# Four edits to the placing of small work in a graph-attention layer: late edges of heavy tiles, a third early q row, a bias column on ScalarE, earlier scans in a sort

## The chip, the cores and the metric

The kernel runs on one core of a Trainium2 chip. The metric is the device time of one execution in microseconds. A core has TensorE (PE: matmuls and transposes), VectorE (DVE), ScalarE (ACT), GpSimd (POOL: here mostly the issue of indirect DMAs, which gather or scatter rows by index) and SyncE (SP: issue of plain DMAs). Each engine works through its own queue of instructions, and semaphores order work between engines.

## The reference

One transformer layer on a sparse graph, in f32, with a residual and a last layer norm around it:

```python
hs = layer_norm(x); ht = layer_norm(h_target)            # 4096 x 512 each
q = (ht @ Wq + bq).reshape(T, 8, 64) / 8.0
k = (hs @ Wk + bk).reshape(S, 8, 64); v = (hs @ Wv + bv).reshape(S, 8, 64)
logits = where(adj[None] != 0, einsum('thd,shd->hts', q, k), -1e30)
ctx = einsum('hts,shd->thd', softmax(logits), v).reshape(T, 512)
h = layer_norm(ht + ctx @ Wo + bo)
h = h + gelu(h @ W1) @ W2                                 # 512 -> 2048 -> 512
out = layer_norm(x + h)
```

`adj` is 4096 x 4096 int32. It holds the diagonal and about 0.4% of other entries, so a target row has 11 to 39 neighbours.

## The kernel before, in words

**Lists instead of dense attention.** The kernel never multiplies 4096 x 4096. For each tile of 128 targets `edges(i)` reads the tile's rows of `adj` in four quarters (SP loads them; ScalarE L740 turns a quarter into flags and counts degrees; VectorE L747 multiplies by a column index and L749 takes maxima of short segments into `cand`, the last of them noted in `maxima`). Then VectorE L756 to L773 decode the candidates into `gid` and take the 24 (`RE`) largest into the target's record `rec`. What stays in `gid` is written to a DRAM table `rest_d` by SP (L780, in `keep_rest`).

**Sorting by degree.** `sort(part)` sorts the records of one half of the targets by falling or rising number of edges: a one-hot matrix (L841), totals on PE (L853), running sums on VectorE (two scans, L859), ranks by a triangular matmul on PE (L870) and VectorE L871 to L874, then 16 scatters by POOL (L878) that write the records to DRAM in sorted order. So every tile of 128 sorted targets has a `cap`, the largest degree in it: 11, 13, 14, 15, 15, 16, 17, 17, 18, 19, 19, 20, 22, 23, 24, 39, then 12, 38, 13, 24 and so on to 18. Tiles 15 and 17, with caps 39 and 38, are the only ones above `RE`: they are the heavy tiles. For them `rest_of(i)` gathers the leftovers back from `rest_d` (POOL, L992, into a new `gid`), and VectorE takes further edges from it, eight at a time (L792 clears those already taken, L793 takes the next eight, twice over), then counts them (L796, L799). `issue(k)` starts `rest_of` when the tile's first gathers are issued, and finishes it before the gathers beyond slot 12.

**Stage 1** (0 to about 276 us). `project` normalises the source rows in 16 groups of 256, transposes them and multiplies by Wk and Wv (L954), and the K|V rows go to a DRAM table `kvd`. Beside it run the lists of the first half, `late_constants` (constants with the biases; PE L662 makes a transposed row, VectorE L665 copies one column of it to `rbc`, which PE uses in a further matmul) and `sort(0)`. At its end `first_fronts` makes the q rows of the first `EARLY` tiles: `front(i)` gathers the targets' rows of `h_target` (L992), normalises (ScalarE L1023), transposes (PE L1035, ScalarE L1038), multiplies by Wq (PE L1045, eight matmuls) and adds the bias (VectorE L1050). For later tiles the same `front` is stepped inside attention, with a VectorE tie (L1027) that keeps it behind the newest logits, and L1030 and L1031 in place of L1025 and L1023.

**Stage 2.** `attention` goes through the 32 tiles in groups of two or one, and through a tile's edges three slots at a time. A slot is one neighbour of each of the 128 targets: POOL gathers its K|V rows (L992) into a ring of 17, later 20 slots. VectorE multiplies keys by q (L1285) and sums per head (L1291), ScalarE takes exp (L1298, L1313, L1263), VectorE weights two slots' values (L1232) and, in some tiles, adds two slots (L1236), ScalarE weights the third (L1266 x8), and PE adds all up by transposing matmuls into PSUM (L1245). `finish` closes a tile (sums L1121 to L1128, ScalarE L1131, PE L1137 to L1155, layer norm with POOL's power L692, ScalarE L1177, PE L1186, ScalarE L1190). `feed` runs the feed-forward network on PE (L1405, L1414) with gelu on ScalarE (L1408). `other_lists` makes the lists of the second half and `sort(1)` in the background.

**What sets the order.** All streams are Python generators; `_weave` interleaves them by the costs that they yield, which gives a program order. A list scheduler of the tile framework then reorders each engine's queue before the kernel runs, so the order on the chip is fixed at build time. `behind(x)` pins what is issued inside it after the last of the instructions in the list `x`: `issues` holds the newest gather, `logits` the newest L1291, `maxima` the newest L749, `newest` the newest ScalarE L1266.

Of the kernel before, what the change touches and what calls it, by code (L numbers as in the profile page):

```python
# [375 lines left out]
MAXE = 40  # L376
RE = 24
DEG, TGT, ROW, RST, E0 = 0, 1, 2, 3, 5
# [65 lines left out]
def adj_resnorm_kernel(  # L444
# [88 lines left out]
    with tc.tile_pool(name="keep", bufs=1) as keep:  # L533
# [17 lines left out]
        with ExitStack() as late:  # L551
# [89 lines left out]
            def late_constants():  # L641


                zero = wp.tile([P, 2 * D // P], F32, name="zero")
                nc.vector.memset(zero, 0.0)
                nc.sync.dma_start(kvd[0:1, :].rearrange("o (p n) -> (o p) n", p=P), zero)
                nc.sync.dma_start(wo, Wo.rearrange("(c p) n -> p c n", p=P))
                nc.sync.dma_start(wq, Wq.rearrange("(c p) n -> p c n", p=P))
                bob = row_bcast(wp, bo, "bob")
                nc.sync.dma_start(bqr, bass.AP(tensor=bq.tensor, offset=bq.offset,  # L650
                                               ap=[[0, P], [1, D]]))
                yield
                yield
                pb = psi.tile([P, D], F32, name="pq", bufs=3)
                for kc in range(KC):
                    nc.tensor.matmul(pb, bvc[:, kc:kc + 1].to_broadcast([P, P]), wo[:, kc, :],
                                     start=kc == 0, stop=kc == KC - 1)
                nc.vector.tensor_add(bob, pb, bob)
                yield
                pt = psi.tile([P, D], F32, name="pq", bufs=3)  # L660
                for kc in range(KC):
                    nc.tensor.transpose(pt[:, kc * P:(kc + 1) * P], bob[:, kc * P:(kc + 1) * P],  # L662
                                        ident)
                rbc = wp.tile([P, KC], F32, name="rbc")
                nc.vector.tensor_copy(rbc.unsqueeze(2), pt.rearrange("p (c t) -> p c t", c=KC)  # L665
                                      [:, :, 0:1])
                nc.vector.tensor_add(b1r, rbc, b1c)
                yield
                pb = psi.tile([P, D], F32, name="pq", bufs=3)
                for kc in range(KC):  # L670
                    nc.tensor.matmul(pb, rbc[:, kc:kc + 1].to_broadcast([P, P]), wq[:, kc, :],
                                     start=kc == 0, stop=kc == KC - 1)
                nc.vector.tensor_sub(bqr, bqr, pb)
                nc.vector.tensor_scalar_mul(bqr, bqr, HD ** -0.5)
# [48 lines left out]
            def behind(ins):  # L723
                return tc.issue_after(ins[-1]) if ins else nullcontext()
# [57 lines left out]
            def rest_of(i):  # L782


                keep_rest()
                rec = recs[i]
                gid = lp.tile([P, 2 * SEG, 8], F32, name="gid")
                flat = gid.rearrange("p s e -> p (s e)")
                gather(flat, rest_d, rec[:, TGT:TGT + 1])
                yield  # L790
                for c in range(E0 + RE, E0 + MAXE, 8):
                    nc.vector.match_replace(flat, rec[:, c - 8:c], flat, 0.0)  # L792
                    nc.vector.max(rec[:, c:c + 8], flat)  # L793
                has = lp.tile([P, MAXE], F32, name="ehas")
                num = lp.tile([P, 1], F32, name="num")
                nc.vector.tensor_scalar(has, rec[:, E0:E0 + MAXE], 0.0, 0.0, op0=ALU.is_gt,  # L796
                                        op1=ALU.add, accum_out=num)
                part = 1 if TILES[i][0] >= PARTS[1][0] * P else 0
                nc.vector.tensor_tensor(bad[:, 6 + part:7 + part], num, rec[:, DEG:DEG + 1],  # L799
                                        ALU.not_equal)  # L800
# [20 lines left out]
            def sort(part):  # L821

                i0, n = PARTS[part]
                me = slice(i0, i0 + n)
                pool, R = lp, Rs[part]
                nc.vector.tensor_reduce(deg[:, me], dpart[:, me, :], AX.X, ALU.add)
                nc.vector.tensor_copy(R[:, :, DEG], deg[:, me])
                dif, rank = tools[:, 928:928 + n], tools[:, 944:944 + n]
                ranki, b16 = tools[:, 960:960 + n].bitcast(I32), tools[:, 976:984].bitcast(BF16)
                nc.vector.scalar_tensor_tensor(dif, deg[:, me], float(RE), cnt[:, me], op0=ALU.min,  # L830
                                               op1=ALU.not_equal)
                nc.vector.tensor_reduce(bad[:, 1 + part:2 + part], dif, AX.X, ALU.max)
                nc.vector.tensor_scalar(dif, deg[:, me], 0.0, float(NB - 1), op0=ALU.max,
                                        op1=ALU.min)
                nc.vector.tensor_scalar(b16, dif, -1.0, float(NB - 1), op0=ALU.mult, op1=ALU.add)
                if part:
                    oh = turn_of("wide", wide).bitcast(BF16)
                else:
                    oh = wp.tile([P, NB * n], BF16, name="oh")
                oh = oh[:, :NB * n].rearrange("p (b i) -> p b i", b=NB)  # L840
                nc.vector.tensor_tensor(oh, b16.unsqueeze(1).to_broadcast([P, NB, n]),  # L841
                                        bins.unsqueeze(2).to_broadcast([P, NB, n]), ALU.is_equal)
                ohf = oh.rearrange("p b i -> p (b i)")
                pos = turn_of("wide", wide).bitcast(F32)
                pos = pos[:, :NB * n].rearrange("p (b i) -> p b i", b=NB)
                posf = pos.rearrange("p b i -> p (b i)")
                w = NB * n // 2
                yield 6.0 if part else 2.0
                tots = []
                for c in range(2):  # L850
                    sl = slice(c * w, (c + 1) * w)
                    pt = ps.tile([P, w], F32, name="t" if part else "cps", bufs=2)
                    nc.tensor.matmul(pt, ones_bf, ohf[:, sl], start=True, stop=True)  # L853
                    tots.append((sl, pt))
                if not part:
                    yield 6.0
                for c, (sl, pt) in enumerate(tots):
                    with behind([] if part else maxima):
                        scan = nc.vector.tensor_tensor_scan(  # L859
                            posf[:, sl], one_c.to_broadcast([P, w]), pt,  # L860
                            0.0 if c == 0 else posf[:, c * w - 1:c * w],
                            op0=ALU.mult, op1=ALU.add)
                while factors:
                    with behind([scan.ins]):
                        factors.pop()()
                yield 4.0
                for c in range(2):
                    sl = slice(c * w, (c + 1) * w)
                    pa = ps.tile([P, w], F32, name="t" if part else "cps", bufs=2)
                    nc.tensor.matmul(pa, lower, ohf[:, sl], start=True, stop=True)  # L870
                    nc.vector.tensor_add(posf[:, sl], pa, posf[:, sl])  # L871
                nc.vector.tensor_mul(pos, pos, oh)
                nc.vector.tensor_reduce(rank, pos.rearrange("p b i -> p i b"), AX.X, ALU.add)
                nc.vector.tensor_copy(ranki, rank)  # L874
                yield 10.0
                for i in range(n):
                    with behind(issues):
                        ins = nc.gpsimd.indirect_dma_start(  # L878
                            out=recs_d[part][:, :],
                            out_offset=bass.IndirectOffsetOnAxis(ap=ranki[:, i:i + 1], axis=0),  # L880
                            in_=R[:, i, :], in_offset=None)

                    tc.declare_no_dep(ins.ins, group=f"scatter{part}", reason="other rows")
                    tc.add_to_no_dep_group(f"scatter{part}", ins.ins)
                    yield 4.5 if part else 1.3
                done.add(part)
# [104 lines left out]
            def gather(dst, table, idx):  # L991
                issues[:] = [nc.gpsimd.indirect_dma_start(  # L992
                    out=dst, out_offset=None, in_=table[:, :],
                    in_offset=bass.IndirectOffsetOnAxis(ap=idx, axis=0)).ins]
# [56 lines left out]
                                               op0=ALU.mult, op1=ALU.add)  # L1051
                tqs[i] = tq

            EARLY = 2

            SG = [(i, j0, min(S, cap - j0)) for i, (_, cap) in enumerate(TILES)
                  for j0 in range(0, cap, S)]
# [524 lines left out]
```

## Time and profile before

| what | value |
|---|---|
| three runs | 1753.59, 1755.61, 1753.04 us (median 1753.59) |
| profiled execution, own time | 1754.37 us |
| its span | 1752.6 us |
| granted TensorE clock, mean | 0.978 |
| busy: PE, DVE, ACT, POOL | 1651.9, 1425.2, 1236.1, 1020.6 us |
| kv gathers (POOL L992) | 603, 784.7 us busy, 1301 ns each |
| matmuls of the feed (L1405, L1414) | 468.8 and 464.8 us busy |
| first feed matmul starts at | 321.42 us |

All positions in microseconds below are counted from the start of the span. In a timeline a line gives start, duration, engine, source line, operation, result and operands, number of instructions; the bracket holds the idle time of that engine just before, and what ended it. In the list of waits a line gives who waited for whom, then the total in us, the number of times and the longest. In the page's 40 slices each digit is a tenth of busy share.

### The profile page before, as it was taken

To read this page: it belongs to the slowest core of one execution; us is meant where nothing else is said; L and a number is where in the kernel's file an instruction comes from. 1 tells how busy PE (TensorE), PEld (TensorE's weight loads), DVE (VectorE), ACT (ScalarE), POOL (GpSimd) and SP (SyncE) were. 2 spreads that over 40 slices of the span, in tenths; PEclk is the share of its full clock that TensorE was granted. 3 is DMA by queue.
4 is the path that set the end of the run, shared out by engine and by line. 5 is a ranking of instruction groups with operands and counts; after the bars stand their busy time and mean duration, and the time that the engine had idled before them with its cause. 6 is when DMAs were issued, how large, how long until landed. Compare 5 with 4: busy or idle time off the path is not lost. (4 is left out here: it accounts for less than half of the span.)

```text
span 1752.6 us, 22726 instructions
## 1 busy us (share of the span) xinstructions
PE 1651.9 (94%) x6978; PEld 1078.3 (62%) x6978; DVE 1425.2 (81%) x2456; ACT 1236.1 (71%) x3135; POOL 1020.6 (58%) x824
## 2 busy tenths in 40 slices
PE   7999996899999999898889999999999999999997
PEld 3444443676676767565567677666666666666665
DVE  6888797889898988997888998988988788999300
ACT  5776663788678977685668888787868677878311
POOL 1000155757666666778777788777887856775101
PEclk9999997999999999998999999999999999999999
DMA  9999988978888887777788888887777767675000
GB/s 353 370 389 361 370 264 286 372 259 284 296 291 297 303 321 256 241 223 246 251 303 292 296 277 314 287 275 237 266 243 242 254 220 257 223 259 191 24 1 27
DMA packets 141610, 461.00 MB, mean 263 GB/s; under 512 B 18036, under 2 KB 23048, under 8 KB 141480
## 3 DMA queue, kind: packets, MB, share of 16 engines
q0 software_dynamic: 96272, 342.33, 57.5%
q1 hardware_dynamic: 39504, 98.26, 15.7%
q10 hardware_dynamic: 5704, 18.89, 2.7%
q8 instruction: 57, 0.93, 0.2%
q14 instruction: 73, 0.60, 0.1%
HBM read 430.61 MB, written 28.79 MB: 262 GB/s over the span
## 5 line engine op out<-in xcount | busy, mean ns | idle before, releaser
L992 POOL DMA_INDIRECT kv<-kvd,rec x603 | 784.7, 1301 | 302.7 <-issue 113.4
L1405 PE MATMUL pf<-h2T,w 128*128 128x256 f32 (+1 forms) x2304 | 468.8, 358 | 5.4 <-ACT h2T L1190 5.4
L1414 PE MATMUL po<-w,gt 128*128 128x512 f32 x1024 | 464.8, 597 | 5.8 <-ACT gt L1408 5.8
L1405 PEld LDWEIGHTS pf<-h2T,w 128*128 128x128 f32 x2304 | 394.4, 191 | 67.0 <-issue 17.9
L1285 DVE TENSOR_TENSOR kv<-kv,tq 128x1536 f32<-128x1536 f32 (+2 forms) x211 | 351.8, 1678 | 54.9 <-DMA kv<-kvd,rec 39.6
L1266 ACT ACTIVATE kv<-kv,pa 128x64 f32<-128x64 f32 x1520 | 390.2, 337 | 3.8
L1291 DVE TENSOR_REDUCE lg<-kv 128x24 f32<-128x1536 f32 (+2 forms) x211 | 350.6, 1669 | 0.4
L1414 PEld LDWEIGHTS po<-w,gt 128*128 128x128 f32 x1024 | 189.1, 192 | 203.9 <-issue 194.6
L1245 PEld LDWEIGHTS cps<-ident,kv 128*128 128x128 f32 x1828 | 219.3, 145 | 112.3 <-issue 46.4
L1245 PE MATMUL cps<-ident,kv 128*128 128x128 f32 x1828 | 244.3, 280 | 45.0 <-DVE kv L1236 24.8
L1232 DVE TENSOR_TENSOR kv<-kv,p 128x1024 f32<-128x1024 f32 (+1 forms) x211 | 251.3, 1195 | 23.9 <-ACT p L1298 22.5
L692 POOL TENSOR_TENSOR n_rs<-n_ve,mhalf 128x2 f32<-128x2 f32 (+2 forms) x53 | 53.8, 1014 | 328.6 <-DVE n_ve L685 155.0
L740 ACT ACTIVATE kv<-kv 128x1024 uint8<-128x1024 int32 x128 | 134.4, 1053 | 61.0 <-DMA kv<-in_adj_dram 22.1
L1408 ACT ACT_TABLE_LOAD x109 | 139.8, 1283 | 1.9
L1408 ACT ACTIVATE gt<-pf 128x512 f32<-128x512 f32 x128 | 76.4, 597 | 75.5 <-PE pf L1405 72.1
L954 PE MATMUL pq<-wk,h2T 128*128 128x512 f32 x256 | 119.5, 609 | 2.5 <-DMA wk<-in_L_gnn_Wk_dram 1.1
L1155 PE MATMUL t<-wo,rb 128*128 128x512 f32 x256 | 117.4, 602 | 4.5 <-DVE rb L1142 4.5
L954 PE MATMUL pq<-wv,h2T 128*128 128x512 f32 x256 | 115.6, 594 | 4.7 <-DVE rbc L665 3.0
L1045 PE MATMUL t<-wq,tq 128*128 128x512 f32 x256 | 115.1, 593 | 1.2 <-ACT tq L1038 1.2
L749 DVE MAX8 cand<-kv 128x8 uint16<-128x171 uint16 (+1 forms) x384 | 108.5, 325 | 1.1
L1298 ACT ACTIVATE p<-lg 128x24 f32<-128x24 f32 (+2 forms) x179 | 39.0, 218 | 82.2 <-DVE lg L1291 79.3
L954 PEld LDWEIGHTS pq<-wv,h2T 128*128 128x128 f32 x256 | 48.4, 190 | 68.0 <-issue 56.5
(165 smaller groups left out, 1593.9 us busy)
## 6 DMA issues: line engine op xcount, KB each, us to landing
kv<-in_adj_dram SPq DMA_DIRECT2D x128, 512.0 KB, 7.0
kvd<-tq ACTq DMA_DIRECT2D x23, 512.0 KB, 6.8
kv<-kvd,rec POOLq DMA_INDIRECT x603, 5.9
kv<-in_L_gnn_h_target_dram SPq DMA_DIRECT2D x32, 256.0 KB, 7.1
w<-in_L_gnn_W_dram SPq DMA_DIRECT2D x8, 1024.0 KB, 8.4
kv<-in_x_dram SPq DMA_DIRECT2D x15, 512.0 KB, 8.4
kvd<-kv ACTq DMA_DIRECT2D x9, 512.0 KB, 6.8
rest_d<-gid SPq DMA_DIRECT2D x32, 96.0 KB, 4.7
```

The source lines that it names most:

```text
L740: nc.scalar.activation(sg, a, AF.Sign, accum_out=dpart[:, i, h:h + 1])
L954: nc.tensor.matmul(pkv, hT[:, kc, j * P:(j + 1) * P], w[:, kc, :], start=kc == 0, stop=kc == KC - 1)
L992: issues[:] = [nc.gpsimd.indirect_dma_start(out=dst, out_offset=None, in_=table[:, :], in_offset=bass.IndirectOffsetOnAxis(ap=idx, axis=0) ...
L1155: nc.tensor.matmul(pa, ct[:, c, :], wo[:, c, :], start=False, stop=c == KC - 1, skip_group_check=True)
L1232: nc.vector.tensor_tensor(v4, v4, p[:, j0:j0 + m, :].unsqueeze(3) .to_broadcast([P, m, H, HD]), ALU.mult)
L1245: nc.tensor.matmul(cps[:, c, :], kv[:, j, D + c * P:D + (c + 1) * P], ident, is_transpose=True, start=j0 + j == 0 and c == 0, stop=j0 + n ...
L1266: newest[:] = [nc.scalar.mul(v, v, pa[:, hd:hd + 1]).ins]
L1285: nc.vector.tensor_tensor(kv[:, :n, :D], kv[:, :n, :D], tq[:, :D].unsqueeze(1) .to_broadcast([P, n, D]), ALU.mult)
L1291: logits[:] = [nc.vector.tensor_reduce(lg[:, :n, :], kv[:, :n, :D].rearrange("p j (h d) -> p j h d", h=H), AX.X, ALU.add).ins]
L1405: nc.tensor.matmul(pf[:, k, :], w1[(f0 + k) // KC][:, kc, (f0 + k) % KC * P:((f0 + k) % KC + 1) * P], h2T[:, kc, :w], start=kc == 0, stop= ...
L1408: nc.scalar.activation(gt, pf, AF.Gelu_apprx_tanh)
L1414: nc.tensor.matmul(po[j], gt[:, k, j * P:(j + 1) * P], w2[(f0 + k) // KC][:, (f0 + k) % KC, :], start=False, stop=f0 + k == FC - 1, skip_g ...
```

## The change

1. The column copy of L665 goes from VectorE to ScalarE.
2. In `rest_of`, the gather of the leftovers is pinned behind the newest gather, and the loop of L792 and L793 behind the newest logits. (In program order they stood there already; before, the scheduler could move them ahead.)
3. In `sort(0)`, the list `maxima` is copied one step sooner, when the totals are multiplied, and the scans are pinned behind that older entry.
4. `EARLY` goes from 2 to 3: the third tile's q row is made in `first_fronts`, with the first two.

```diff
@@ late_constants
-                nc.vector.tensor_copy(rbc.unsqueeze(2), pt.rearrange("p (c t) -> p c t", c=KC)
+                nc.scalar.copy(rbc.unsqueeze(2), pt.rearrange("p (c t) -> p c t", c=KC)
                                       [:, :, 0:1])
@@ rest_of
-                gather(flat, rest_d, rec[:, TGT:TGT + 1])
-                yield
-                for c in range(E0 + RE, E0 + MAXE, 8):
-                    nc.vector.match_replace(flat, rec[:, c - 8:c], flat, 0.0)
-                    nc.vector.max(rec[:, c:c + 8], flat)
+                with behind(issues):
+                    gather(flat, rest_d, rec[:, TGT:TGT + 1])
+                yield
+                with behind(logits):
+                    for c in range(E0 + RE, E0 + MAXE, 8):
+                        nc.vector.match_replace(flat, rec[:, c - 8:c], flat, 0.0)
+                        nc.vector.max(rec[:, c:c + 8], flat)
@@ sort
-                tots = []
+                tots, held_by = [], list(maxima)
@@ sort
-                    with behind([] if part else maxima):
+                    with behind([] if part else held_by):
                         scan = nc.vector.tensor_tensor_scan(
@@ front, after it
-            EARLY = 2
+            EARLY = 3
```

Counts of instructions stay as they were, but for those of the edited lines and two table loads of ScalarE fewer. In the built order of the changed kernel, the leftovers' gathers stand at the start of tiles 15 and 17 on POOL, after kv gathers 267 and 316 (before: after 184 and 257); the L792 loops stand at the start of those tiles on VectorE; on PE both L870 stand ahead of the next Wk matmuls of L954 (before, they were two matmuls apart); and the third tile's L1035 and L1045 stand ahead of the first L1245. From L791 on, the line numbers of the changed kernel are higher by two.

## The prediction

> **What bounds the kernel now.** I read the page first (busy shares, then the 40 slices), then TensorE's list of waits, then the timeline around each long wait.
>
> ```profile
> span 1752.6 us, 22726 instructions
> PE 1651.9 (94%) x6978; PEld 1078.3 (62%) x6978; DVE 1425.2 (81%) x2456; ACT 1236.1 (71%) x3135; POOL 1020.6 (58%) x824
> PE   7999996899999999898889999999999999999997
> PEclk9999997999999999998999999999999999999999
> ```
>
> TensorE is busy 94% of the span, and the idle rest is 1752.6 - 1651.9 = 100.7 us. The PE row shows where: the start, slice 7 (about 263 to 307 us, where the list and projection stage turns into attention), and slices 17 and 19 to 21 (701 to 745, 789 to 920 us). From about 920 us on it is full. So PE's work sets the end, and an edit is worth what it takes out of PE's idle time, plus the slow matmuls that follow it. PE's list of waits gives the causes:
>
> ```profile
> PE cps L1245 <- DVE kv L1236: 24.8, 4, 8.4
> PE cps L1245 <- DVE kv L1232: 20.0, 5, 6.3
> PE pq L954 <- DVE rbc L665: 3.0, 1, 3.0
> PE cps L870 <- DVE kv L859: 3.0, 1, 3.0
> ```
>
> The first two rows are attention matmuls waiting for VectorE to weight the value rows. The last two are what two of the four edits aim at. The timeline around one L1236 wait shows its origin:
>
> ```profile
> 695.83 0.99 POOL L992 DMA_INDIRECT gid<-rest_d,rec  x1 [3.23 <-DMA rest_d<-gid]
> 698.51 0.09 DVE L792 MATCH_VALUE_LOAD gid<-rec,gid 128x8 int32 x1 [5.91 <-DMA gid<-rest_d,rec]
> ...
> 712.02 1.97 PE L1245 MATMUL cps<-ident,kv 128*128 128x128 f32 x8 [7.16 <-DVE kv L1236]
> 713.40 2.78 POOL L992 DMA_INDIRECT kv<-kvd,rec  x1 [6.52 <-PE cps L1245]
> ```
>
> A write of leftover edges to DRAM (issued by SP at 690.19) has to land before POOL may gather `gid`; the gather lands at 698.5; VectorE's queue stands 5.91 us with the L792 loop at its head; 13 us later PE runs dry, and POOL, which needs PE to free a ring slot, stands 6.52 us.
>
> **What the Trainium skill says.** "TensorE: Matmul & The Clock Gate" bears on this three ways. Its opening table has VectorE as strict FIFO: an early-placed wait blocks everything behind it. The 5.91 us agree. Part 1 ("The HAM clock gate") says that an idle window of about 3.4 us halves PE's clock. Here, after 7.16 us idle, eight L1245 matmuls take 1.97 us, against 1.04 at 901.42: agrees, so a long stall costs about 1 us more than itself. "DMA: Bandwidth & Descriptors" (Anatomy of one DMA) gives a gather about 2.0 us fixed; `gid` takes 2.7 from issue to landing here. "ScalarE activation tables: per-element evaluation and per-set limits" (What a function is on this engine) prices a table load at 1283 ns; the trace has 1283 as mean of 109.
>
> **Part 1, heavy tiles (L780 to L799).** Moved for tile 15 (cap 39): one POOL gather and VectorE's L792/L793 twice plus L796 and L799, from 692 to 701 us to the tile's own start near 884 (gather) and 905 to 917 (loop). Tile 17 (cap 38): gather from about 868, loop from 895 to 945, both to about 950 to 1005. Counts do not change.
> - *Removed at 692 to 713.* VectorE's wait 5.91, and ahead of the next logits 0.43 (L792 with its load), 0.36 (L793), 0.43 (L792) = 1.22; together 7.1 us earlier. PE's 7.16 wait goes with it (what it waits for comes at 711.96 - 7.1 = 704.86, when PE finished its last matmul), and POOL's ring wait ends near 705.9. Clock recovery adds up to 0.9 (1.97 - 1.04).
> - *Does it survive?* From 713 to 915 POOL is the pace, not PE: about 16 us busy of every 20, plus 0.30 issue ahead of each of 12 to 16 instructions, which fills the stretch; VectorE waits there on gathers that have just landed (9.75 at 803.18, 4.83 at 860.65). Since POOL too starts 7.5 earlier, I move the whole pattern by 7 to 7.5. SP's queue is passed by one adjacency load, whose buffer has slack. After 920 PE is 279.1 of 280 busy, so a shift there reaches the end.
> - *New at tile 15.* VectorE waits at 912.74 for 2.43, so one pair of L792/L793 (0.79) hides. The second pair stands ahead of L1232 at 914.57, which ends PE's 5.61 us wait at 915.83: +0.8. Behind VectorE's loop are queued L1232 and the next logits. The new gather (1.29 with issue) puts POOL's next kv gathers back; it is not seen in the trace there. Bounds: 0, if it falls in POOL's 3.50 idle before 917.22, and 1.3 + 2.7 = 4.0, if VectorE meets the loop just when it is issued. I take 0: in the changed kernel's order the gather stands after kv gather 267, about 20 us ahead of the loop.
> - *Tile 17.* Two pairs, up to 2.0 us of VectorE, where PE has 2.0 and 3.8 us of other work in hand: 0. That work is the cover.
> Sum: -7.5 + 0.8 = **-6.7**, bounds -8.5 and -2.5.
>
> **Part 2, third q row (EARLY 2 to 3).** The gather of its row, ScalarE's L1023 (0.76) and L1038 x4 (1.45), PE's L1035 x4 (0.60) and L1045 x8 (3.60), VectorE's L1050 (0.69) move from 312 to 334 to before the first logits; one L1027, L1030, L1031 each becomes the early form (L1031 about 0.8 on ScalarE). The place they go to is idle:
>
> ```profile
> 283.13 1.22 DVE L1285 TENSOR_TENSOR kv<-kv,tq 128x1024 f32<-128x1024 f32 x1 [4.92 <-DMA kv<-kvd,rec]
> 287.18 1.97 PE L1245 MATMUL cps<-ident,kv 128*128 128x128 f32 x8 [6.31 <-DVE kv L1232]
> ```
>
> PE is idle 6.31 there and then 3.80, 2.15, 2.15, so 4.2 us of matmuls become free; at 321.96 and 330.41 they stood behind the feed's start, on PE's path: -4.2. Tile 0's q is later by about 1.7 (two PSUM buffers, now for three tiles), from 277.52 to 279.3, hidden by the wait for gathers to 283.13. VectorE is the pace from there to 308: +0.69 (L1050), part of it against the 0.28 and 0.29 waits for exp; with the later landing for the second group (287.7) I take +1.1 at the feed's start. A kv gather put ahead of the pow (L692) costs 0 to 1.25. Of the -3 some comes back at PE's 4.36 wait (462.97, for L1142), since VectorE there waits on gathers. Two table loads go too (2 x 1.28, off the path). I take **-2**, bounds -4.2 and +1.5.
>
> **Part 3, bias column (L665).** PE waits 2.99 for `rbc`:
>
> ```profile
> 132.52 3.70 PE L954 MATMUL pq<-wv,h2T 128*128 128x512 f32 x8 [2.99 <-DVE rbc L665]
> ```
>
> ScalarE ends a copy of L956 at 131.2 and can do rbc by 131.5: PE restarts 1.0 earlier. But at 203.3 the stage meets x's loads again (VectorE L702 idle 3.15 for `in_x`, ScalarE L915 idle 8.11; DMA busy shares are near full in 80 to 200 us), which are in no hurry because of PE. I take **0**, bounds -1 and +0.5 (if ScalarE's copy delays the next L956).
>
> **Part 4, scans (L859).** The scans go from behind four adjacency quarters to behind the second and third: about 212.65 and 214.75 for their ends, from 215.81 and 216.92.
>
> ```profile
> 215.86 0.32 PE L870 MATMUL cps<-oh,lower 128*128 128x384 bf16 x1 [2.98 <-DVE kv L859]
> ```
>
> Both L870 now stand ahead of the next wk matmuls, so PE waits for the second scan: about 0.7 + 1.9 = 2.6 instead of 2.98, and the four wk matmuls after it, 3.34, come nearer the 1.7 of a full clock. So 0.4 to 1.9 on PE. Stage 1 however ends by its list chain: ScalarE's L740 waits 4.03 (240.69) and 4.33 (266.35) for adjacency loads, and the last kvd rows land at 276.4, where the first kv gather (276.46) starts. List work pushed behind the sort delays one SP write (220.86) by some 2 us; the cover is the ring of adjacency buffers. I take **0**, bounds -2 and +1.
>
> **Sum:** -6.7 - 2 = -8.7 against the profiled execution, 1754.37 us (span 1752.6 plus 1.77 around it): 1745.7. The three runs have median 1753.59, 0.78 below it, so 1744.9; **1745**.
>
> **The rivals.**
> - *Partly given back* (0.2): POOL, already the pace from 713 to 915, does not start its gathers earlier by all of 7.5, because other releases (landings, record loads near 865.63, 5.19 idle) come at their own time; and the new wait at tile 15 costs 2. For it: in five of the ten stretches of 20 us from 720 to 920 PE is already not full. Against: what POOL waits for is itself released by POOL's own scatters and gathers. -3 - 1: 1749 to 1752.
> - *Everything* (0.13): -8.5, -4.2, -1, -1.5, all carried: about 1738.5. Against: 462.97 and 203.3.
> - *Stall moved, slower* (0.10): VectorE meets the loop before `gid` has landed, at tile 15 and again at tile 17, which had it free before. Price 7.1 each as at 698.51; against the 7.2 saved and EARLY's -2 it decides from a sum of 9.2 on; in full, 14.2 - 9.2 = +5: 1758.5. For: strict order on VectorE. Against: the writes have landed 190 us before, and the gather leads the loop by several kv gathers.
> - *The scans edit does not do what it says* (no time of its own): PE waits as long, for the second scan.
> My case has 0.57. Range 1738.5 to 1752: it leaves out the stall moved and a few mishaps. About 0.2%, 3.5 us, is what a measurement of this kernel can tell from no change; faster means below 1750.1. Faster: 0.57 + 0.13 + a third of the 0.2 = 0.77; same 0.13; slower 0.10.
>
> **What would show it.** Right: no 5.91 wait at L792, no PE wait near 705 to 712, rows of 803 and 913 some 9 us earlier with the same waits; PE's wait near 281 shorter by 4, the q matmuls at 330 gone; the PE idle sum near 92. Wrong: a wait for `gid` at L792 in tile 15 or 17; POOL's pattern from 740 on unmoved; the first feed (321.42) later by over 2 us; last kvd rows after 277.

## The result, and the profile after

| | before | after |
|---|---|---|
| median of 22 runs each | 1755.55 us | 1751.10 us |
| ratio, 95% interval | | 0.9977 (0.9966 to 0.9987) |
| profiled execution: span | 1752.6 us | 1751.8 us |
| PE busy in it | 1651.9 us | 1657.4 us |

The change makes the kernel faster by 0.23% (0.13 to 0.34%), 2.3 to 6.0 us, where 8.7 us had been forecast: the sign was right, the size not. A repeat beside other kernels gave 0.9980 (0.9968 to 0.9992). In both series single executions of one kernel lie 8 to 18 us apart, so the two spans above say almost nothing: PE's busy time for the same 6978 matmuls alone differs from trace to trace, from 1647.5 (h_only_tie) to 1661.2 us (e_h_tie). The comparison of stretches further down says more.

From the page of the changed kernel, span, busy times and two rows of the slices:

```profile
span 1751.8 us, 22710 instructions
PE 1657.4 (95%) x6978; PEld 1080.6 (62%) x6978; DVE 1424.3 (81%) x2454; ACT 1233.9 (70%) x3134; POOL 1022.9 (58%) x824
PE   7999896899999999998789999999999999999997
PEclk9999998899999999999899999999999999999998
```

The digit of slice 17 is now 9, where it was 8: the stall at 712 is gone. Slice 20 (832 to 876 us) went from 8 to 7. From its list of TensorE's waits (who waited for whom: total, times, longest):

```profile
PE cps L1247 <- DVE kv L1234: 19.4, 6, 8.3
PE cps L1247 <- DVE kv L1238: 15.5, 3, 8.5
...
PE cps L872 <- DVE kv L861: 2.3, 2, 1.6
...
PE pq L956 <- ACT rbc L665: 1.3, 1, 1.3
```

The wait for `rbc` went from 3.0 to 1.3, that for the scans from 3.0 to 2.3, that for L1238 (L1236 before) from 24.8 to 15.5. Waits for ScalarE grew: that of L1047 (a tile's q matmul) for L1040 from 1.2 to 3.5, that of L1037 (the transposes of a q row) for L1033 from 0.5 to 2.5, and that of L1188 (the transposes of the normalised h) for L1179 from 3.3 to 5.5.

The timeline of the changed kernel around the old stall, and then the leftovers' gather and loop in their new places:

```profile
694.71 3.43 DVE L1287 TENSOR_TENSOR kv<-kv,tq 128x1536 f32<-128x1536 f32 x2
...
706.58 1.09 PE L1247 MATMUL cps<-ident,kv 128*128 128x128 f32 x8
```

```profile
875.68 3.49 POOL L994 DMA_INDIRECT gid<-rest_d,rec  x1 [0.30 <-issue]
```

```profile
902.75 0.08 DVE L794 MATCH_VALUE_LOAD gid<-rec,gid 128x8 int32 x1
902.82 0.34 DVE L794 MATCH_REPLACE8 gid<-rec,gid 128x192 f32<-128x192 f32 x1
...
908.82 2.82 PE L1247 MATMUL cps<-ident,kv 128*128 128x128 f32 x12 [5.90 <-DVE kv L1234]
```

VectorE's 5.91 us wait is gone, and so is PE's 7.16 (L1247 at 706.58 has no bracket). The L794 loop finds its data landed: no bracket either. PE's wait at tile 15 is 5.90, 0.29 longer than before.

**Stretch by stretch.** The matmuls of the feed's first layer (L1405 before, L1407 after; 2304 of them, counted from 0) are milestones that stand in the same order in every kernel. The table gives, from one trace of each kernel, the time from the first kv gather to milestone 448, then from 704 to 768 (about 701 to 761 us), 768 to 1024 (to 964) and 1024 to 1152 (to 1059). The columns after the name say which edits a kernel has; "pin" and "relief" are explained with their experiments.

| kernel | heavy | EARLY 3 | to 448 | 704-768 | 768-1024 | 1024-1152 |
|---|---|---|---|---|---|---|
| before | | | 244.1 | 60.1 | 202.8 | 94.7 |
| rs_only | | | 245.9 | 58.3 | 202.7 | 95.3 |
| e_only | | x | 244.9 | 60.1 | 200.8 | 95.6 |
| b_relief | | | 246.4 | 57.9 | 203.3 | 95.9 |
| h_only | x | | 247.9 | 52.8 | 201.3 | 103.4 |
| h_loop | loop only | | 246.4 | 51.9 | 203.2 | 103.2 |
| after | x | x | 244.7 | 52.6 | 201.5 | 105.3 |
| after_again | x | x | 245.7 | 51.2 | 204.9 | 101.1 |
| h_only_tie | x, pin | | 243.8 | 51.7 | 204.4 | 99.3 |
| after_tie | x, pin | x | 242.6 | 51.9 | 202.3 | 101.3 |
| e_h_tie | x, pin | x | 244.2 | 53.3 | 205.1 | 98.9 |
| e_loop_tie | loop, pin | x | 244.7 | 53.1 | 203.3 | 104.8 |
| h_relief | x, relief | | 249.2 | 52.3 | 202.8 | 97.3 |
| h_tie_relief | x, pin, relief | | 245.9 | 51.2 | 201.4 | 94.3 |

Means: from 704 to 768, 59.1 without the heavy edit and 52.2 with it, so 6.9 gained; from 768 to 1024, 202.4 and 203.0, so 0.6 lost; from 1024 to 1152, 95.4 without it and 103.3 in the four that have it with neither pin nor relief, so **7.9 lost again**. That last column is where the forecast gain went. It stays lost: between milestones 1152 and 1376 no kernel's place, measured against the mean of the four without the heavy edit, moves by more than 3 us. The end points matter, though: most of the loss stands between milestones 1151 and 1152, about 1043 to 1062 us, where PE has other work than the feed's first layer; a column that ended at 1151 would miss it.

**What PE waits for there.** The kernel before has waits of 0.3 and 0.2 us between 957 and 1064 us. The changed kernel's list of PE's waits for that stretch is:

```profile
PE t L1047 <- ACT tq L1040: 2.8, 1, 2.8
PE t L1188 <- ACT h L1179: 2.4, 2, 2.0
PE t L1037 <- ACT tq L1033: 2.2, 1, 2.2
```

All three are waits for ScalarE, none for a gather directly. The second leads back to POOL: L1179 normalises h, and needs a power that POOL makes (L692), in the same queue as the gathers. The power and the first transpose, before and then in the changed kernel:

```profile
1043.72 0.73 POOL L692 TENSOR_TENSOR n_rs<-n_ve,mhalf 128x2 f32<-128x2 f32 x1
1045.78 0.27 PE L1186 MATMUL t<-ident,h 128*128 128x128 f32 x1
```

```profile
1043.93 0.73 POOL L692 TENSOR_TENSOR n_rs<-n_ve,mhalf 128x2 f32<-128x2 f32 x1
1045.77 0.33 PE L1188 MATMUL t<-ident,h 128*128 128x128 f32 x1 [2.03 <-ACT h L1179]
```

PE comes 2 us sooner (its matmul ahead of these ends at 1043.73, before at 1045.94), POOL does not. This power starts 3.2 to 5.6 us after VectorE has made its input in the four traces without the heavy edit, 6.2 to 7.6 us in the eight with it and no relief, and 2.5 us in the two with heavy edit and relief. An exp ahead of L1179 in ScalarE's queue comes late as well: it waits for sums whose key product waited 2.75 us for a gather. From milestone 1024 to 1152 PE is idle for 0.5 to 1.6 us in the four without the heavy edit, 4.9 to 8.5 in the four with neither pin nor relief, 3.0 to 5.7 in the four with the pin, 2.9 with the relief and 0.2 with both. The rest of the loss is matmuls that run slower after a wait: seven L1188 at 1046.47 take 1.76 us, seven L1186 before 0.98.

### The profile page after: what moved, and what is told of

It is laid out like the page before. It is cut to its first block, busy times and chain, and to the rows that moved or that the text cites. A ratio compares the mean times of both kernels' runs of the same rounds, so it can differ in the third digit from the quotient of the medians.

```text
span 1751.8 us, 22710 instructions
## 1 busy us (share of the span) xinstructions
PE 1657.4 (95%) x6978; PEld 1080.6 (62%) x6978; DVE 1424.3 (81%) x2454; ACT 1233.9 (70%) x3134; POOL 1022.9 (58%) x824
## 5 line engine op out<-in xcount | busy, mean ns | idle before, releaser
L994 POOL DMA_INDIRECT kv<-kvd,rec x603 | 797.2, 1322 | 303.9 <-issue 114.8
L1407 PE MATMUL pf<-h2T,w 128*128 128x256 f32 (+1 forms) x2304 | 469.8, 358 | 3.5 <-ACT h2T L1192 3.4
L1407 PEld LDWEIGHTS pf<-h2T,w 128*128 128x128 f32 x2304 | 395.9, 192 | 64.9 <-issue 17.9
L1293 DVE TENSOR_REDUCE lg<-kv 128x24 f32<-128x1536 f32 (+2 forms) x211 | 350.4, 1668 | 0.2
L1416 PEld LDWEIGHTS po<-w,gt 128*128 128x128 f32 x1024 | 189.1, 192 | 202.3 <-issue 194.8
L1247 PEld LDWEIGHTS cps<-ident,kv 128*128 128x128 f32 x1828 | 218.1, 144 | 101.9 <-issue 47.1
L1247 PE MATMUL cps<-ident,kv 128*128 128x128 f32 x1828 | 243.0, 279 | 35.0 <-DVE kv L1234 19.4
L692 POOL TENSOR_TENSOR n_rs<-n_ve,mhalf 128x2 f32<-128x2 f32 (+2 forms) x53 | 53.3, 1006 | 336.5 <-DVE n_ve L685 172.7
L1047 PE MATMUL t<-wq,tq 128*128 128x512 f32 x256 | 116.7, 600 | 3.5 <-ACT tq L1040 3.5
```

The lines of the kernel that those rows point to most:

```text
L994: issues[:] = [nc.gpsimd.indirect_dma_start(out=dst, out_offset=None, in_=table[:, :], in_offset=bass.IndirectOffsetOnAxis(ap=idx, axis=0) ...
L1247: nc.tensor.matmul(cps[:, c, :], kv[:, j, D + c * P:D + (c + 1) * P], ident, is_transpose=True, start=j0 + j == 0 and c == 0, stop=j0 + n ...
L1293: logits[:] = [nc.vector.tensor_reduce(lg[:, :n, :], kv[:, :n, :D].rearrange("p j (h d) -> p j h d", h=H), AX.X, ALU.add).ins]
L1407: nc.tensor.matmul(pf[:, k, :], w1[(f0 + k) // KC][:, kc, (f0 + k) % KC * P:((f0 + k) % KC + 1) * P], h2T[:, kc, :w], start=kc == 0, stop= ...
L1416: nc.tensor.matmul(po[j], gt[:, k, j * P:(j + 1) * P], w2[(f0 + k) // KC][:, (f0 + k) % KC, :], start=False, stop=f0 + k == FC - 1, skip_g ...
```

## The experiments

Two theories were put against each other. **A**: POOL's gathers are the pace (what sets when everyone else can go on) not only to 915 but to about 1060 us. **T**: the pinned loop of tile 17 pushes another small VectorE instruction back.

**h_only** has the second edit alone (`behind(issues)` and `behind(logits)` in `rest_of`); **h_loop** only the pin of the loop, with the gathers where the scheduler puts them (after kv gathers 184 and 283).

> Heavy-tile edit alone. Theory A (POOL's gathers are the pace from 713 to about 1060 us, not only to 915, and the moved gid gathers, 3.8 and 1.7 us with issue in the trace of the changed kernel, now stand inside that stretch): -7.5 at 755 us, most of it gone by 1062, net -2 to -5 us against the kernel before. Rival B (the heavy edit keeps its -6.7, and the other edits cost 2 to 3): -6.7 (-5.5 to -8). A wait of PE at L1247 around 712 is absent in both.

> Only VectorE's L792/L793 loop is pinned behind the logits; the gid gathers stand where the scheduler puts them, after kv gathers 184 (as before) and 283. Theory A: the first gather's 3.8 us leave the paced stretch, while its wait for the rest_d writes falls before 713, where POOL had 6.5 us idle: 1.5 to 4 us faster than h_only. Rival B: the gather's place costs nothing, so h_loop is equal to h_only, or 1 slower because POOL stands 3.2 us at 692.

Measured: h_only 1.0007 of before (0.9995 to 1.0019), h_loop 0.9993 (0.9984 to 1.0002). The heavy edit alone brings nothing, less than the 2 to 5 us that A still left it. Rival B falls. That h_loop is faster than h_only is not clear from these intervals; its stretch 1024 to 1152 is as long (103.2), though no `gid` gather lies in it. So the moved gathers are not the main loss, against what A said of them.

**e_only** is `EARLY = 3` alone, **rs_only** the first and third edits alone.

> EARLY = 3 alone. The prediction on record: -2. From the trace of the changed kernel: the third tile's 4.2 us of PE work is gone from behind the feed's start, but the feed starts 1.3 later by the new order and its first 64 matmuls take 9.6 us instead of 7.3 on a cold clock: about -0.5 (-2 to +2). Rival: the order of the first gathers costs more than the trace shows, +2 to +3.

> Bias column on ScalarE and earlier scans alone. The prediction on record: 0 (-3 to +1.5). In the trace of the changed kernel the first kv gather starts 1.4 later than before (277.8 against 276.5), which is either chance of that execution (then 0) or the price of the list work pushed behind the sort (then +1.4).

Measured: e_only 0.9982 (0.9968 to 0.9995), about -3.2 us; rs_only 1.0012 (0.9998 to 1.0027). The third q row is worth its forecast 2 us or a little more, and is the only one of the three parts that gains alone. The first kv gather starts between 274.0 and 280.3 in the ten traces without the first and third edits (mean 277.8) and between 276.7 and 279.6 in the four with them (277.9): nothing speaks for the 1.4 us seen after being more than chance.

**The pin on a tie.** In the q path of tile 18 VectorE first makes a tie (L1027 before, L1029 after), ScalarE's L1033 waits for it, and PE's L1037 for that. In the order of the changed kernel the tie stands one key product later than before. VectorE's and PE's timelines of the changed kernel:

```profile
1054.34 1.76 DVE L1287 TENSOR_TENSOR kv<-kv,tq 128x1536 f32<-128x1536 f32 x1 [3.88 <-DMA kv<-kvd,rec]
1056.02 1.75 DVE L1293 TENSOR_REDUCE lg<-kv 128x24 f32<-128x1536 f32 x1
1058.01 1.23 DVE L1287 TENSOR_TENSOR kv<-kv,tq 128x1024 f32<-128x1024 f32 x1 [0.25 <-DMA kv<-kvd,rec]
1059.15 0.22 DVE L1029 SCALAR_TENSOR_TENSOR rec<-rec,lg 128x2 f32<-128x2 f32 x1
```

```profile
1060.69 0.66 PE L1037 MATMUL t<-ident,tq 128*128 128x128 f32 x4 [2.24 <-ACT tq L1033]
```

The tie needs the newest sums, L1293 at 1056.02. They stand behind a key product that waits 3.88 us for its gather, and a second product with a wait is put between the sums and the tie. In h_loop, with the pin of the loop alone, PE waits 2.7 us at this place too, so it is the loop's pin that moved the tie. The kernels with "tie" in their name add one pin; nothing else in any engine's order changes but VectorE's near that place:

```diff
 # front(i)
+                    if i == 18:
+                        tied[:] = [tie.ins]
 # attention, ahead of the next key product
-                            with behind(closing[:1 if j0 < 2 * S else 2]):
+                            with behind(tied or closing[:1 if j0 < 2 * S else 2]):
 # after it: tied.clear()
```

> The whole change, and one pin more: VectorE's tie for tile 18 (L1029 of the changed kernel) ahead of the next key product L1287. Theory T: the pinned loop of tile 17 pushed that tie one key product later in VectorE's order, behind a product that waits 4 us for its gather; PE's L1037 waits for it (2.2 to 3.9 us at 1056 to 1060) and then runs on a cold clock, so the heavy edit's gain is lost there. T expects no PE wait at L1037 there and 3 to 6 us less than the changed kernel: ratio to before 0.994 to 0.996. Theory A (POOL's gathers are the pace, whatever VectorE's order): no gain, 0.9977 as the changed kernel; PE would stand a few us later at the next gather instead.

> The heavy edit alone with the same pin on tile 18's tie. Theory T: -3 to -6 against h_only, so -4 to -7 against before, near the -6.7 on record. Theory A: as h_only, 0 to -1.5.

> EARLY = 3, the loop pinned with the gid gathers left to the scheduler, and the pin on tile 18's tie; bias column and scans as before. If the parts add up (EARLY -3.2, h_loop -1.2, tie -5): -8 to -10 against before, faster than after_tie by 1 to 3. Theory A: -4 to -5.

> The changed kernel once more on the chip of the other three, for a second trace and a direct comparison: 0.9977 of before (-4), PE at the feed's 1152nd L1407 matmul 8 to 11 us later against the kernel before than at its 1024th (the loss at 964 to 1062 us is of the order, not of one execution). If the loss was chance of one execution, it is absent here.

Measured: after_tie 0.9986 (0.9971 to 1.0001), h_only_tie 0.9978 (0.9955 to 1.0000), e_loop_tie 0.9965 (0.9948 to 0.9983), after_again 0.9980 (0.9968 to 0.9992). In after_tie's trace the pin does locally what T said; its lines are one to three higher:

```profile
1049.28 0.22 DVE L1030 SCALAR_TENSOR_TENSOR rec<-rec,lg 128x2 f32<-128x2 f32 x1
```

```profile
1053.72 0.62 PE L1040 MATMUL t<-ident,tq 128*128 128x128 f32 x4
```

No wait is left at these transposes, in any kernel with the pin. What that is worth is not settled. after_tie is not faster than the changed kernel, against T; h_only_tie is 5 us faster than h_only by their ratios, as T said, but the two intervals overlap a little; e_loop_tie gained 6.1 us, between what A and T expected. The last column of the table is 101.1 on the mean of the four kernels with the pin and no relief, against 103.3, and PE's idle time there 4.7 against 7.0, but the single values overlap. So T explains some 2 of the 8 us, as far as the scatter lets one say. The loss itself repeats (after_again 101.1, after 105.3, with 94.7 before), though after_again's 6 us are less than the 8 to 11 expected.

**The relief.** Nine gathers of POOL go to SP, five of them between 890 and 1060:

```diff
+                            if g in (8, 9, 10):
+                                nc.sync.dma_start(xt, x[i * P:(i + 1) * P, :])
+                            else:
                                 ... (the gather, as before)
 # front: the same with h_target for tiles 17 to 19
```

> h_only with nine of POOL's gathers taken over by plain DMAs of SP: the x rows of the tile groups fed near 1012 us and later (L994, xt) and the h_target rows of tiles 17 to 19 (tq). SP takes unsorted rows, so those rows of the output are other rows than the reference's; the orders of PE, VectorE and ScalarE stay word for word. Five of the nine lie before 1060, 9 us of POOL in h_only's trace. Theory A (POOL is the pace to 1060): the loss of PE between its 1024th and 1152nd L1407 matmul, 8.7 in h_only, shrinks to 0 to 4, and the whole is 4 to 8 faster than h_only. Theory T (only the order of tile 18's tie): the loss stays above 6, the whole within 2 of h_only.

> The kernel before with the same nine gathers on SP (the same rows unsorted). PE is full there from 920, so both theories expect little: 0 to -2.5 at the 1152nd matmul (one gather of the five lies before 920, where PE still waits). If it gains as much as h_relief does, POOL's relief is worth as much without the heavy edit, and A's reading (that the heavy edit's gain is what POOL withholds) falls.

> h_only with both the nine gathers on SP and the pin on tile 18's tie. If A and T are both part of the cause, the loss between the 1024th and the 1152nd matmul is gone (-1 to +2), and the heavy edit keeps its full gain: -7 to -9 against b_relief.

Measured against before: h_relief 1.0036 (1.0021 to 1.0051), b_relief 1.0055 (1.0038 to 1.0072), h_tie_relief 1.0024 (1.0011 to 1.0038). All three have about 17 us of span after the start of the last scatter, where the kernel before has 7.2. Of these 10 us, 9.85 lie in two instructions that close POOL's queue (INC_SWDGE_SEM 2.35 us against 0.42, DRAIN 8.89 against 0.97), with the same lengths in all three traces and the short ones in the other eleven; why, the runs do not show. They come after the last work, so less 9.85 us of 1758.5 (an estimate from these traces) the ratios would be 0.9980 for h_relief, 0.9999 for b_relief and 0.9968 for h_tie_relief.

In the last column of the table the relief takes the heavy edit's loss from 7.9 to 1.4 (h_relief 97.3 against b_relief 95.9), and relief and pin together leave none (94.3). Without the heavy edit it brings nothing there (95.9 against 94.7 to 95.6). Medians agree in part: h_tie_relief 1762.08 against b_relief's 1767.67, -5.6 us of the 7 to 9 expected, while h_relief, with 1765.73, has only -1.9, and its interval overlaps b_relief's. By the estimate h_relief is some 4.7 us faster than h_only, within A's 4 to 8. The busy times by stretch of h_only and then of h_tie_relief show it (length; PE, PEld, DVE, ACT and POOL with counts; granted clock; DMA share; GB/s):

```profile
1000.00:1040.00 40.00, 39.62 (x193) 28.64 (x191) 36.45 (x36) 29.07 (x89) 32.65 (x24) 1.00 0.80 270
1040.00:1080.00 40.00, 34.26 (x156) 24.72 (x157) 31.76 (x35) 26.82 (x80) 26.62 (x24) 0.91 0.86 296
```

```profile
1000.00:1040.00 40.00, 40.00 (x189) 28.44 (x188) 40.00 (x42) 31.90 (x97) 27.10 (x23) 1.00 0.87 305
1040.00:1080.00 40.00, 37.32 (x197) 27.57 (x196) 34.07 (x37) 29.34 (x89) 29.86 (x24) 1.00 0.83 296
```

With POOL's time cut from 32.65 to 27.10, VectorE is busy 40.00 of 40 instead of 36.45, and PE's hole at 1040 to 1080 shrinks from 5.7 to 2.7. A holds, for the pace, on one trace of each kernel; the pace is set by POOL's total time, whichever gathers are moved. Two other causes can be set aside. The transfers themselves were not the limit: the relieved kernel moves more (305 GB/s against 270), and kv gathers 312 to 360 land a median 5.8 to 6.2 us after their start with the heavy edit, 5.9 to 6.1 without, in the ten traces that record it. And the scheduler's other changes of order by the heavy edit, in VectorE's and ScalarE's queues, stand in h_tie_relief as well, which loses nothing.

**e_h_tie** is after_tie without the first and third edits.

> The change without its first and third edit (bias column on VectorE, scans held as before), with the pin on tile 18's tie: after_tie less those two edits. If the two edits cost the 2 us that rs_only's median had, this is 2 faster than after_tie was (0.9986): about 0.9975. If they cost nothing, as on record, it is 0.9986, and the difference of after_tie to e_loop_tie (0.9965) is that of the gid gathers' place.

Measured: 0.9969 (0.9953 to 0.9984), nearer to the first reading. rs_only and this comparison both put 2 to 3 us on the bias and scan edits, but each interval reaches zero, and no stretch of the traces shows them. That stays open. e_h_tie and e_loop_tie have the lowest ratios, 0.9969 and 0.9965, and beat the kernel before; against the changed kernel's 0.9977 and 0.9980 their intervals overlap.

## Why the prediction was right or wrong

- **Heavy tiles, what is removed:** right. 7 to 7.5 forecast, 6.9 on the mean of the traces, and PE's wait at 712 went with VectorE's.
- **Heavy tiles, does it survive to 920:** right, as far as the scatter of some 2 us in that column lets one see. From 768 to 1024 the loss is 0.6; the forecast 0.8 at tile 15 can't be told from it.
- **The step that failed: "After 920 PE is 279.1 of 280 busy, so a shift there reaches the end".** PE was full there in the kernel before, but POOL was as good as full too: kv gathers 312 to 360 are 92 us with 1.9 us of idle time beyond issue. (VectorE, with 258 of the 280 us busy, was not far off.) Two engines were level. When PE came 7 us sooner, POOL took 95 to 98 us for the same gathers in the eight traces with the heavy edit and no relief; VectorE waited for gathers, ScalarE for VectorE and POOL's power, and PE for ScalarE. A busy engine shows that it bounds at its present place in time, not that it may be moved. The 7.9 us that came back are the mis-sized term; forecast was 0. The rival "partly given back" had the mechanism, but put it at 713 to 915 and at -3. That the measured 1751.10 us lies where this rival had put it, and inside the stated range, is in part luck: the kernel before had a median of 1755.55 in the longer series, 2 us above the 1753.59 that the sum started from.
- **Tile 17 "0":** wrong. The loop of 2 us itself was covered, as forecast, but it made the scheduler put tile 18's tie one key product later. The pin gives back perhaps 2 of the 7.9. This is what a list scheduler's order has to be read for: not where the edited instructions go, but which others they push.
- **The gid gather:** I took 0 for POOL's time. It took 3.49 at 875.68, for it started beside a product (below). That h_loop hardly differs says that its place matters little.
- **Third q row:** right in the sum. Forecast -2; alone -3.2 (-5.6 to -0.9); the mean of "to 448" is 246.2 us in the eight kernels without it and 244.5 in the six with it, -1.7. The tile's q matmuls do fill idle time, but not the wait that was named: the first L1247 comes 6.8 us later after the first gather than before, and its wait is 8.27, not 6.31 less 4. The waits that follow are shorter. From the first gather to the feed's start PE is idle for 19.9 us on the mean of the eight and 16.9 of the six. In the changed kernel:

```profile
276.50 10.57 PE L1047 MATMUL t<-wq,tq 128*128 128x512 f32 x24 [0.74 <-ACT tq L1040]
295.34 1.97 PE L1247 MATMUL cps<-ident,kv 128*128 128x128 f32 x8 [8.27 <-DVE kv L1234]
...
324.66 9.64 PE L1407 MATMUL pf<-h2T,w 128*128 128x128 f32 x64
```

- **Bias column and scans:** 0 forecast. The waits fell by 1.7 and 0.7 us, and the end of stage 1 did not move, as said; a cost of 2 us is not excluded. Both L872 wait for their scans, 0.66 and 1.63 us, close to the prediction's 0.7 and 1.9 and less than the 2.98 of before, which the fourth rival would have left. (The upper bound of that part adds up to 2.0, not 1.9.)
- **Sum of parts:** by their ratios the parts alone are +1.2, -3.2 and +2.1 us, together +0.1; the whole was -4.0 and -3.5. The intervals (1.8 to 2.5 either way) allow it, but I don't claim that the parts add up.
- **"Stall moved":** did not happen; VectorE never met the loop before `gid` had landed.
- **The signs that were named:** the 5.91 and 7.16 us waits are gone and the q matmuls at 330 too, as forecast; PE's idle sum fell to 94.4 in one trace of the changed kernel and was 100.3 in the other, where 92 was expected. Two signs of being wrong showed up: the first feed matmul came at 324.66, 3.2 us later, of which 1.4 is the later first gather, and the first gather, which had started where the last kvd rows landed, started at 277.82, after 277. Neither points to the step that failed. One reading was loose: PE ran dry at 704.86, 6.4 us after the leftovers' gather had landed; 13.5 us after it PE went on.

## What to carry to other kernels

Before a saving is carried to the end because the last stretch is full on one engine, look whether a second engine in that stretch is full as well: its queue, its issue time and what holds it. Compare executions by milestones of one engine, not by spans: a 7 us effect was plain in every trace while spans differed by 17 (21 with the relief). Look at several milestones, since one can stand on the wrong side of a hole. And read a scheduler's new order for the bystanders of an edit, not for the edit alone.

## What the runs showed of the hardware

POOL's gathers lengthen beside VectorE's products. In the trace before, a kv gather that starts while VectorE runs L1285 or L1232 (both operands in SBUF) takes 1.82 us on the mean (221 of them); the other 382 take 1.00. Of those held, the middle half ends 0.81 to 0.83 us after VectorE's instruction does, as if most of its 0.94 us began only then; in the changed kernel it is the same (1.86 and 1.00). Beside L1291 (a sum) or L1142 (one operand in PSUM) a gather takes 0.94 to 0.95. POOL's and VectorE's timelines of h_only show two such cases:

```profile
1013.27 3.51 POOL L994 DMA_INDIRECT xt<-in_x_dram,tags  x1 [0.30 <-DVE rb L1144]
1017.08 0.94 POOL L994 DMA_INDIRECT kv<-kvd,rec  x1 [0.30 <-PE cps L1247]
1018.33 3.44 POOL L994 DMA_INDIRECT kv<-kvd,rec  x1 [0.30 <-issue]
```

```profile
1013.07 1.75 DVE L1287 TENSOR_TENSOR kv<-kv,tq 128x1536 f32<-128x1536 f32 x1
1014.74 1.22 DVE L1234 TENSOR_TENSOR kv<-kv,p 128x1024 f32<-128x1024 f32 x1
1015.87 1.74 DVE L1293 TENSOR_REDUCE lg<-kv 128x24 f32<-128x1536 f32 x1
1017.53 3.41 DVE L1287 TENSOR_TENSOR kv<-kv,tq 128x1536 f32<-128x1536 f32 x2
```

Each long gather ends 0.8 us after the products it started beside. The Trainium skill, "SBUF — State Buffer" (Who interferes with whom), says that a VectorE instruction with two SBUF inputs contends with a GpSimd instruction that reads SBUF; the figures here agree. They do not agree with the remark in the same section that a probe's `tensor_tensor` did not stall a DMA: here it does. It may be one reason why POOL did not follow when VectorE came sooner. From kv gather 328 to 344 the time above 0.95 us per DMA is 5.7 us in the three traces with none of the heavy edit, pin and relief, and 8.5 to 11.0 in the eight with the heavy edit and no relief; but with one gather more two of the three have 8.8, so the difference hangs on where the count ends. That this is the cause of the pace, or even of its change, is not shown; a kernel whose products take one operand from PSUM was not tried.
